# An earlier page fetch, two pools in the other order, and eleven vector instructions on GpSimd, in a chained conditioning, LoRA and paged-attention kernel

## The chip, the cores and the metric

The kernel runs on one core of a Trainium2 chip. The core has engines with a queue of instructions each, which run at the same time and wait for each other through semaphores: TensorE (PE, matrix products and transposes through the identity; its weight loads are listed as PEld), VectorE (DVE), ScalarE (ACT), GpSimd (POOL) and SyncE (SP, which here issues transfers). An engine takes its own queue strictly in order. The metric is the time of one execution in device microseconds (us), the median of several runs; lower is better.

## The reference, cut to what matters

Activations `x` of shape (64, 32, 512) pass four residual layers in float32: a per-sample channel mix, a linear layer with a per-sample LoRA adapter, grouped-query attention over a paged cache, and a second channel mix.

```python
x = x + einsum('bct,bcd->bdt', x, W0[cond])
x = x + (einsum('bsd,od->bso', x, base_w) + base_b + (x @ A[ad]) @ B[ad])
q, k, v = x @ Wq, x @ Wk, x @ Wv            # 32 query heads, 8 key/value heads, 128 each
q, k = rope(rmsnorm(q), pos), rope(rmsnorm(k), pos)
k_all = concat([k_cache[block_table], k])   # 16 pages of 32 rows, then 32 new rows
v_all = concat([v_cache[block_table], v])
scores = where(valid, q @ k_all.T / sqrt(128), -1e30)
x = x + softmax(scores) @ v_all @ Wo
x = x + einsum('bct,bcd->bdt', x, W3[cond])
```

The 64 samples with 32 rows each are 2048 rows of 512.

## The kernel before, in words

**Tiles and steps.** The 2048 rows are 16 tiles `t` of 128 rows (4 samples each). The 8 key/value heads are two groups of 4. A step is one group and one tile, 32 in all; a unit is one sample of a step, 128 in all. A unit has 4 scores (one for each key/value head), and each of these takes one slot of a schedule that is written out by hand: `slot(i)` (L1208) says in which order the work due in slot i is put into the engines' queues. Slots 0 to 511 hold attention. Negative slots hold the layers before it: `First` works on one row tile every two slots, and the first pair of steps is projected beside it.

**Registering.** `at(slot, where, ...)` (L948) registers work for a slot, and `run(slot, where)` puts it out. In each slot the order is "fetch", "pool", the scores of that slot, "out", "pe", "take", "late", "power", a piece of the norm list (`norm_piece`), "turn", "dve", two more pieces, "dve" again, "keep", "act" and "store".

**First layers.** For a tile t, `First` (L387) gathers rows of the tables through GpSimd, mixes and applies the linear layer on TensorE, transposes the result (`turn_out`, `keep_out`) and stores it for later pairs. For each odd t, `sums` (L499) forms four half tiles of 128x256 from the transposed tiles of t-1 and t: the operands `x_12` and `x_34` of a seven-product block multiplication. They are stored by `store_sums`; from tile 13 on, these stores go out on GpSimd's queue (`queue`, L514).

**Projection and norm.** `Block` (L637) multiplies a pair of tiles with a block of weights in seven products. Each of a pair's ten query and key results passes through `Norm` (L708): squares on ScalarE, the power -1/2 on GpSimd (`power`, L723 and L725), then four pieces on VectorE, `scale` (L730), `straight` (L737), `swapped` (L749, two halves) and `sum` (L759), which adds the two rotated parts `rot_a` and `rot_b`. When `sum` has been put out, `norm_piece` (L961) registers the transposition `turn` (L764, `head_ps`) for a later slot, and `keep` copies it to SBUF as qT or kT_new. There are two `rot_a` buffers and one `rot_b` buffer.

**A unit.** Making a `Unit` (L781) asks for the 16 pages of its transposed keys: SP loads page numbers (L794) and issues 16 transfers of 64 KB (L802) into one of two `kT` buffers. `mask` (L817) makes the penalty `pen` of 128x544 on GpSimd. `fetch_values` (L105) gathers the values `v_sb` in four pieces by GpSimd. `scores` (L846, L849) multiplies queries and keys; VectorE adds `pen` and takes the extremum (L854, `sm` and `top`); ScalarE takes the exponential (L865) and the division (L871). `flip` (L888, `pT_ps`) transposes the result, and `values` (L898) multiplies it with the values. Units 0 and 1 are made in slots `ready` and `ready + 3`, with `ready = -6` (L1071); the mask of unit 0 is due in slot -2.

**Pools.** SBUF memory is taken in pools that are opened and closed like a stack. `start` (page rows of the cache and the angles) closes in slot `ready - 1`, and the `kT` pool opens on what it leaves. `first` (all that `First` uses, with the last `x_12` and `x_34`) closes in slot -2; then `pages`, `v`, `attn` (with `pen`, `sm`, `pT`) and the PSUM pool `o` open. A tile in reused memory waits until every earlier user of that memory is done, stores out of it included. Transfers signal on eight semaphores for each kind of queue, which are used in turn.

Of the kernel before, what the change touches and what calls it, by code (L numbers as in the profile page):

```python
# [30 lines left out]
ALU = mybir.AluOpType  # L31
# [14 lines left out]
NT = B * S // P  # L46
# [31 lines left out]
def resid_kernel(  # L78
# [19 lines left out]
    nc = tc.nc  # L98

    def across(ap, n):  # L100

        return bass.AP(tensor=ap.tensor, offset=ap.offset, ap=[[0, P], [1, n]])
# [42 lines left out]
    def rows_of(pool, name, source, n, size, lanes, times=1.0, first=0.0, tag=None):  # L145

        i = pool.tile([P, n], I32, name=name, tag=tag or name)
        for c in range(0, n, 64):
            m = min(n - c, 64)
            f = wpool.tile([P, 64], F32, name=f"{name}_f", tag="w11")  # L150
            nc.vector.tensor_scalar(
                f[:, :m], source[:, c : c + m], float(size), lanes, ALU.mult, ALU.add
            )
            nc.vector.tensor_scalar(i[:, c : c + m], f[:, :m], times, first, ALU.mult, ALU.add)
        return i
# [71 lines left out]
    with ExitStack() as l2:  # L227
# [11 lines left out]
        room = {}  # L239
# [6 lines left out]
        lo, hi = slice(0, NC // 2), slice(NC // 2, NC)  # L246
# [140 lines left out]
        class First:  # L387
# [38 lines left out]
            def add(self):  # L426
                nc.vector.tensor_tensor(self.x, self.ps, lora["bias"], ALU.add)
# [43 lines left out]
            def own_ranks(self):  # L471
                self.hT = first_pool.tile([P, P], F32, name="hT", bufs=2)
                nc.vector.tensor_tensor(self.hT, self.h, lora["mask"][self.t % 2], ALU.mult)
# [25 lines left out]
            def sums(self):  # L499

                p = self.t // 2
                pool = first_pool if p else proj_pool
                a, b = first_of[self.t - 1].x2T, self.x2T
                s = pool.tile([P, NC, P], F32, name="x_12")
                nc.vector.tensor_tensor(s[:, lo], b[:, lo], b[:, hi], ALU.add)
                nc.vector.tensor_tensor(s[:, hi], s[:, lo], a[:, lo], ALU.subtract)
                r = pool.tile([P, NC, P], F32, name="x_34")
                nc.vector.tensor_tensor(r[:, lo], a[:, lo], b[:, lo], ALU.subtract)
                nc.vector.tensor_tensor(r[:, hi], a[:, hi], s[:, hi], ALU.subtract)
                self.s = s, r  # L510
                if p == 0:
                    pair_of[0].x["12"], pair_of[0].x["34"] = s, r
# [18 lines left out]
        def with_identity():  # L531

            lora["eye"] = first_pool.tile([P, S], F32, name="eye")
            nc.vector.tensor_tensor(lora["eye"], ident[:, :S], ident[:, S : 2 * S], ALU.add)
            for j in range(2, NB):
                nc.vector.tensor_tensor(
                    lora["eye"], lora["eye"], ident[:, j * S : (j + 1) * S], ALU.add
                )

        def base_chunk(c):  # L540
            part = lora["base"][:, c, c * P : (c + 1) * P]
            nc.vector.tensor_tensor(part, part, ident, ALU.add)
# [165 lines left out]
        class Norm:  # L708
# [46 lines left out]
                        ALU.mult,  # L755
                    )

            def sum(self):
                nc.vector.tensor_tensor(self.a, self.a, self.b, ALU.add)  # L759

            def turn(self):
                self.tp = ps_t.tile([P, REP, P], F32, name="head_ps", tag="t")
# [185 lines left out]
        def at(slot, where, do, *args):  # L948
            plan.setdefault((slot, where), []).append((do, args))

        def run(slot, where):
            for do, args in plan.pop((slot, where), ()):
                do(*args)
# [7 lines left out]
        def norm_piece(slot):  # L961


            if not pieces or pieces[0][0] > slot or busy.get(slot, 0) >= 2 + (slot % 4 == 1):
                return
            busy[slot] = busy.get(slot, 0) + 1
            _, piece, norm = pieces.pop(0)
            piece()
            if norm:
                slot += 1  # L970
                while slot in turning:
                    slot += 1
                turning.add(slot)
                at(slot, "turn", norm.turn)
                at(slot, "keep", norm.keep)
# [92 lines left out]

        n = KG * len(units)
        begin = -WINDOW - AHEAD - 9  # L1070
        ready = -6  # L1071
        for t in range(NT):
            home = -WINDOW - AHEAD - 6 + 2 * t
            f = [first_of, t]
# [133 lines left out]
        def slot(i):  # L1208
# [30 lines left out]
            run(i, "late")  # L1239
            run(i, "power")  # L1240
            norm_piece(i)
            run(i, "turn")
            if i >= 0:
                run(i, "dve")
            norm_piece(i)
            norm_piece(i)
            run(i, "dve")
            run(i, "keep")
# [4 lines left out]
        with tc.manual_schedule(engines=ENGINES):  # L1253

            lora["base"] = first_pool.tile([P, NC, HID], F32, name="base_sb")
            for c in range(NC):
                nc.scalar.dma_start(out=lora["base"][:, c, :], in_=base_w[:, c, :])
            with_identity()
            adapt_sb = first_pool.tile([P, NT // 2], I32, name="adapt_sb")
            for i in (0, 1):  # L1260
                nc.sync.dma_start(
                    out=adapt_sb[i * P // 2 : (i + 1) * P // 2, :],
                    in_=bass.AP(
                        tensor=ints.tensor,
                        offset=ints.offset + I_ADAPT + i,
                        ap=[[2 * N_INT, P // 2], [2, NT // 2]],
                    ),
                )
            nc.sync.dma_start(out=table, in_=ints[:, I_TABLE:])
            lora["rows"] = rows_of(first_pool, "lora_rows", adapt_sb, NT // 2, RANK, lane16_f)  # L1270

            lora["bias"] = first_pool.tile([P, HID], F32, name="bias_sb")
            slot(begin)
            more = angles()
            next(more)
            nc.gpsimd.dma_start(out=lora["bias"], in_=across(base_b, HID))
            for i in range(begin + 3, begin + 15):
                for _ in range(1 + (begin + 5 < i < begin + 11)):
                    at(i, "store", next, more, None)
            for j in (0, 1):  # L1280
                at(begin + 4, "store", load_kv_weights, 0, 1, j)
                at(begin + 5, "store", load_kv_weights, 0, 0, j)
            for c in range(2 * KG):
                at(begin + 8 + c, "store", load_q_weights, 0, c // 2, c % 2)
            for i in range(begin + 1, begin + 11):
                slot(i)
                if i == begin + 2:
                    lora["mask"] = [own_ranks(0), own_ranks(1)]
                    for c in range(NC):
                        base_chunk(c)  # L1290
                if i == begin + 8:
                    nc.vector.tensor_copy(seq_f, ints_sb[:, I_SEQ : I_SEQ + B])
                    key_i = wpool.tile([P, LA], I32, name="key_i", tag="w9")
                    nc.gpsimd.iota(key_i, pattern=[[1, LA]], base=0, channel_multiplier=0)
                    nc.vector.tensor_copy(key_f, key_i)
                    nc.vector.memset(key_f[:, L:], -BIG)
                    v_rows = rows_of(const, "v_rows", table, B * NC, PSIZE, lane32_f)
            for i in range(begin + 11, n + VLAG):
                if i == ready - 1:
                    start.close()  # L1300
                    room["kT"] = l2.enter_context(tc.tile_pool(name="kT", bufs=2))
                if i == -2:
                    first.close()
                    pages = ExitStack()
                    room["pages"] = pages.enter_context(
                        tc.tile_pool(name="pages", bufs=1, side="right")
                    )
                    room["v"] = l2.enter_context(tc.tile_pool(name="v", bufs=2))
                    room["attn"] = l2.enter_context(tc.tile_pool(name="attn", bufs=2))
                    room["o"] = l2.enter_context(tc.tile_pool(name="ps_o", bufs=1, space=PSUM))  # L1310
                if i == SLOTS * NT + 8:
                    pages.close()
                if i == n - 27:
                    assert not pieces
                    proj.close()
                    o_pools.append(
                        ctx.enter_context(tc.tile_pool(name="o_first", bufs=1, side="right"))
                    )
                slot(i)
            run(n + VLAG, "store")  # L1320
# [7 lines left out]
    with ExitStack() as l3:  # L1328
# [34 lines left out]
        lo, hi = slice(0, HALF), slice(HALF, HID)  # L1363
# [162 lines left out]
```

## Time and profile before

| what | value |
|---|---|
| median of 3 runs | 2446.4 us (2442.44 to 2447.73) |
| the profiled execution's own time | 2447.26 us |
| its span in the profile | 2445.4 us |
| PE busy | 2402.6 us, 98% of the span |
| DVE / ACT / POOL busy | 1649.4 / 1400.8 / 1231.0 us |
| PE busy in 160 to 200 us | 17.46 + 16.50 of 40 us |

The span runs from the first to the last instruction of the program; 1.86 us of the execution lie around it. A line of a timeline gives the start in us, the duration in us, the engine, the source line, the operation, the tiles written and read, how many were merged, and in brackets the engine's idle time before it with what ended that. The end of one line's work may overlap the start of the next on TensorE, where products are pipelined. Attention's slot 0 begins at 181.61 us of the span.

### The profile page before, as it was taken

The page shows a single profiled execution, that of the slowest core. Times are in us where ns is not written, and L with a number is a line of the kernel's source. Part 1 is how long each engine was busy: PE and PEld are TensorE (multiplying, and loading weights), DVE is VectorE, ACT ScalarE, POOL GpSimd, SP SyncE. Part 2 cuts the span into 40 slices and gives each one's busy share as a digit, 9 for nine tenths or more (in the row PEclk, how much of TensorE's full clock was granted, in tenths as well). Part 3 has the DMA queues.
Part 4 walks back from the last instruction along what each step waited for, and adds up shares of the span by engine and source line. Part 5 has one row for each costly group of instructions (what it writes and reads, how often), then busy time and mean ns, then how long its engine had stood idle before and what let it go on. Part 6 is the DMA issues. An engine that isn't in the chain of part 4 may idle for free.

```text
span 2445.4 us, 47109 instructions
## 1 busy us (share of the span) xinstructions
PE 2402.6 (98%) x13792; PEld 1865.4 (76%) x13792; DVE 1649.4 (67%) x3555; ACT 1400.8 (57%) x4005; POOL 1231.0 (50%) x1266
## 2 busy tenths in 40 slices
PE   7999999999999999999999999999999999999999
PEld 4657777777777777777777777777777788888887
DVE  5557777777777777787777777777787756333222
ACT  2246777777777777767777777767677653000000
POOL 3336566656665667665665666566556653000000
PEclk9999999999999999999999999999999999999999
DMA  8776666666766677766666656666667774233221
GB/s 270 250 228 196 192 191 200 190 204 184 207 183 203 189 215 235 235 186 193 173 188 177 189 175 187 178 186 182 181 181 226 248 245 147 105 113 130 87 89 59
DMA packets 461680, 452.09 MB, mean 185 GB/s; under 512 B 67889, under 2 KB 384177, under 8 KB 457841
## 3 DMA queue, kind: packets, MB, share of 16 engines
q1 hardware_dynamic: 405920, 268.95, 36.6%
q0 software_dynamic: 54928, 179.09, 24.3%
q8 instruction: 111, 1.82, 0.3%
q14 instruction: 145, 1.18, 0.2%
q10 hardware_dynamic: 576, 1.05, 0.1%
HBM read 380.73 MB, written 76.55 MB: 187 GB/s over the span
## 4 chain that ended last, share of the span: by engine, by line
PE 92%; DMA 3%; issue 2%; DVE 1%; ACT 1%; SPq 1%; POOL 1%; ACTq 0%; POOLq 0%; DVEq 0%
PE proj_ps L662 22%; PE o_ps L898 17%; PE out_ps L1350 15%; PE s_ps L846 9%; PE pT_ps L888 9%; PE s_ps L849 8%; PE l_ps L479 3%; PE head_ps L764 3%; PE o_ps L911 1%; DMA kT<-kT 1%; DMA o<-oT 1%; PE s_ps L881 1%; SPq L802 1%; PE h_ps L463 1%; PE mix_ps L1368 1%
## 5 line engine op out<-in xcount | busy, mean ns | idle before, releaser
L105 POOL DMA_INDIRECT v_sb<-v,v_rows x512 | 544.2, 1063 | 362.9 <-PE o_ps L898 253.9
L898 PE MATMUL o_ps<-pT,v_sb 128*128 128x128 f32 x4096 | 624.6, 275 | 3.0 <-DVE pT L890 3.0
L898 PEld LDWEIGHTS o_ps<-pT,v_sb 128*128 128x128 f32 x4096 | 577.7, 191 | 32.0 <-DVE pT L890 5.4
L865 ACT ACTIVATE sm<-sm,top 128x544 f32<-128x544 f32 x512 | 380.8, 744 | 332.3 <-DVE top L854 240.7
L854 DVE CUSTOM_DVE_ANT_0 sm<-s_ps,pen 128x544 f32<-128x544 f32 x512 | 369.3, 721 | 112.4 <-PE s_ps L849 99.2
L871 ACT ACTIVATE sm<-sm,share 128x512 f32<-128x512 f32 x512 | 369.8, 722 | 110.5 <-DVE share L870 73.6
L890 DVE COPY pT<-pT_ps 128x512 f32<-128x512 f32 x512 | 353.2, 690 | 66.8 <-PE pT_ps L888 16.3
L846 PE MATMUL s_ps<-kT,qT 128*128 128x288 f32 x1024 | 334.9, 409 | 3.4 <-DMA kT<-kT 1.9
L888 PE MATMUL pT_ps<-ident,sm 128*128 128x128 f32 x2048 | 310.1, 274 | 5.2 <-ACT qT L776 3.7
L674 DVE TENSOR_TENSOR raw<-proj_ps,raw 128x512 f32<-128x512 f32 x332 | 224.4, 688 | 129.3 <-PE proj_ps L662 117.2
L849 PE MATMUL s_ps<-kT,qT 128*128 128x256 f32 x1024 | 304.7, 379 | 4.9 <-issue 2.8
L846 PEld LDWEIGHTS s_ps<-kT,qT 128*128 128x128 f32 x1024 | 179.2, 190 | 151.2 <-issue 127.8
L817 POOL TENSOR_SCALAR pen<-key_f,seq_f 128x544 f32<-128x544 f32 x128 | 283.9, 2218 | 12.5 <-DMA kT<-kT 1.2
L888 PEld LDWEIGHTS pT_ps<-ident,sm 128*128 128x128 f32 x2048 | 239.2, 142 | 9.4 <-ACT qT L776 4.9
L718 ACT ACTIVATE sq<-raw 128x128 f32<-128x128 f32 x640 | 198.5, 310 | 74.0 <-DVE raw L674 56.1
L849 PEld LDWEIGHTS s_ps<-kT,qT 128*128 128x128 f32 x1024 | 194.5, 190 | 59.4 <-issue 5.9
L105 POOL DMA_INDIRECT mix_rows<-in_w,cond_rows x32 | 36.0, 1126 | 349.8 <-DVE mix_diag L170 301.2
L870 DVE RECIPROCAL share<-total 128x1 f32<-128x1 f32 x512 | 83.8, 164 | 180.4 <-ACT sm L865 152.2
L723 POOL TENSOR_SCALAR ss<-ss 128x4 f32<-128x4 f32 x160 | 40.1, 251 | 312.1 <-ACT sq L718 305.9
L1400 ACT COPY p<-out_ps 128x256 f32<-128x256 f32 x7 | 2.6, 373 | 333.1 <-PE out_ps L1350 333.1
L662 PE MATMUL proj_ps<-sum,x 128*128 128x512 f32 x380 | 188.0, 597 | 0.0
L725 POOL TENSOR_TENSOR rstd<-ss,minus_half 128x4 f32<-128x4 f32 x160 | 168.6, 1054 | 13.4
(172 smaller groups left out, 3572.0 us busy)
## 6 DMA issues: line engine op xcount, KB each, us to landing
kT<-kT SPq DMA_DIRECT2D x2048, 64.0 KB
o_in<-o SPq DMA_DIRECT2D x28, 1024.0 KB
o<-oT POOLq DMA_DIRECT2D x69, 256.0 KB
o<-oT SPq DMA_DIRECT2D x58, 256.0 KB
page_rows<-in_kv_cache SPq DMA_DIRECT2D x32, 256.0 KB
v<-in_kv_cache SPq DMA_DIRECT2D x32, 256.0 KB
kT<-page_rows SPq DMA_DIRECT2D x32, 256.0 KB
vn<-raw SPq DMA_DIRECT2D x32, 256.0 KB
```

Source lines behind the costliest of these rows:

```text
L105: nc.gpsimd.indirect_dma_start(out=dst, out_offset=None, in_=table, in_offset=bass.IndirectOffsetOnAxis(ap=index, axis=0),)
L662: nc.tensor.matmul(self.ps, lhsT=self.pair.x[x][:, c if x == "b" else half.start + c, :], rhs=blocks(self.b)[w][:, c, :], start=(c == 0), ...
L817: nc.gpsimd.tensor_scalar(self.pen, key_f, seq_f[:, self.b : self.b + 1], BIG, ALU.is_ge, ALU.mult)
L846: nc.tensor.matmul(ps[:, first:HID], lhsT=q, rhs=self.kT[:, :n1, k, :], start=True, stop=True)
L849: nc.tensor.matmul(ps[:, HID : first + LA], lhsT=q, rhs=self.kT[:, n1:, k, :], start=True, stop=True)
L854: nc.vector.tensor_tensor_reduce(out=sm, in0=ps[:, first : first + LA], in1=self.pen, scale=1.0, scalar=3e38, op0=ALU.add, op1=ALU.min, ac ...
L865: nc.scalar.activation(sm, sm, AF.Exp, bias=top, scale=-1.0, accum_out=total)
L871: nc.scalar.activation(sm[:, :L], sm[:, :L], AF.Copy, scale=share)
L888: nc.tensor.transpose(ps[:, c, :], self.sm[k][:, c * P : (c + 1) * P], ident)
L890: nc.vector.tensor_copy(pT, ps)
L898: nc.tensor.matmul(o_of[self.s, k][:, self.j, :], lhsT=self.v[c][:, k * D : (k + 1) * D], rhs=self.pT[k][:, c, :], start=(self.j == 0 and ...
L1350: nc.tensor.matmul(ps[:, :HALF], lhsT=o[:, i, :], rhs=w[i // REP][:, i % REP, :], start=(i == 0), stop=(i == KG * REP - 1),)
```

## The change

There are four edits.

1. `sums` runs on GpSimd for the last tile (t = 15): four instructions of 128x256. For the other tiles it stays on VectorE.
2. The rotated sum of a `Norm` is put on GpSimd when it is put out in a slot below -1. In the program built from the changed source this is so for seven of the first pair's ten.
3. `ready` becomes -8: unit 0's keys are asked for in slot -8, unit 1's in slot -5, and the `start` pool is closed, and `kT` opened, in slot -9.
4. The `attn` pool is opened before the `v` pool.

```diff
             def sums(self):
...
                 a, b = first_of[self.t - 1].x2T, self.x2T
+                add = (nc.vector if self.t < NT - 1 else nc.gpsimd).tensor_tensor
                 s = pool.tile([P, NC, P], F32, name="x_12")
-                nc.vector.tensor_tensor(s[:, lo], b[:, lo], b[:, hi], ALU.add)
-                nc.vector.tensor_tensor(s[:, hi], s[:, lo], a[:, lo], ALU.subtract)
+                add(s[:, lo], b[:, lo], b[:, hi], ALU.add)
+                add(s[:, hi], s[:, lo], a[:, lo], ALU.subtract)
                 r = pool.tile([P, NC, P], F32, name="x_34")
-                nc.vector.tensor_tensor(r[:, lo], a[:, lo], b[:, lo], ALU.subtract)
-                nc.vector.tensor_tensor(r[:, hi], a[:, hi], s[:, hi], ALU.subtract)
+                add(r[:, lo], a[:, lo], b[:, lo], ALU.subtract)
+                add(r[:, hi], a[:, hi], s[:, hi], ALU.subtract)
...
-            def sum(self):
-                nc.vector.tensor_tensor(self.a, self.a, self.b, ALU.add)
+            def sum(self, engine):
+                engine.tensor_tensor(self.a, self.a, self.b, ALU.add)
...
             _, piece, norm = pieces.pop(0)
-            piece()
+            if norm:
+                piece(nc.gpsimd if slot < -1 else nc.vector)
+            else:
+                piece()
...
-        ready = -6
+        ready = -8
...
+                    room["attn"] = l2.enter_context(tc.tile_pool(name="attn", bufs=2))
                     room["v"] = l2.enter_context(tc.tile_pool(name="v", bufs=2))
-                    room["attn"] = l2.enter_context(tc.tile_pool(name="attn", bufs=2))
```

In the built program the queues read, around the change, as follows. SP: the 16 page transfers of unit 0 stand ahead of the reload of `x_12` (L588) instead of behind it, and those of unit 1 ahead of the reload of `x_34`. GpSimd, from the power of the eighth norm on: power (L723, L725), rotated sum, four x sums, store of the transposed tile 15, two stores of its sums, power, `pen` of unit 0, first gather of values, power, rotated sum, three more gathers, `pen` of unit 1. Before, the same queue reads without the two rotated sums and the four x sums. ScalarE: the first load of the exponential's table (part of L865) is put behind the wait for unit 0's first `top`; before, it stood ahead of that wait.

## The prediction

> **What bounds the kernel now.** I read the page first, then the busy time by stretches, then the idle times of TensorE (PE) in order of time, then GpSimd's timeline. The page has PE busy for 98% of the span and for 92% of the chain that ended last. The stretches (length, then busy us of PE, PEld, DVE, ACT, POOL with their counts, then clock, DMA share, GB/s) show where the edits can matter:
>
> ```profile
> 160.00:180.00 20.00, 17.46 (x65) 8.75 (x64) 16.29 (x33) 8.24 (x31) 8.46 (x14) 1.00 0.54 177
> 180.00:200.00 20.00, 16.50 (x82) 11.61 (x83) 14.79 (x36) 12.17 (x27) 16.95 (x17) 1.00 0.75 220
> ...
> 400.00:500.00 100.00, 99.99 (x619) 77.01 (x619) 75.99 (x169) 72.98 (x211) 62.55 (x64) 1.00 0.65 190
> ```
>
> PE has 6.04 us without work between 160 and 200 us, and 0.01 us between 400 and 500. PE's timeline names the idle times at the entry to attention:
>
> ```profile
> 172.99 0.63 PE L764 MATMUL head_ps<-ident,rot_a 128*128 128x128 f32 x4 [0.48 <-DVE rot_a L759]
> ...
> 176.96 1.98 PE L662 MATMUL proj_ps<-wv,x_a 128*128 128x512 f32 x4 [1.62 <-DVE raw L674]
> 179.05 0.63 PE L764 MATMUL head_ps<-ident,rot_a 128*128 128x128 f32 x4
> 181.61 0.72 PE L846 MATMUL s_ps<-kT,qT 128*128 128x288 f32 x2 [1.93 <-DMA kT<-kT]
> ...
> 189.19 0.63 PE L888 MATMUL pT_ps<-ident,sm 128*128 128x128 f32 x4 [1.37 <-issue]
> ```
>
> They are 0.48 us for a rotated sum, 1.62 us for VectorE, 1.93 us for unit 0's keys, and 1.37 us at 189.19, plus 0.45 us at 186.64 and 0.10 us in small: 5.95 us. That is all that the edits can win here. Every other thing that PE waits for later comes from its own chain, so **what delays PE here delays the end one for one**. The second queue to read is GpSimd's at the same place, since three edits touch it:
>
> ```profile
> 173.36 0.51 POOL L723 TENSOR_SCALAR ss<-ss 128x4 f32<-128x4 f32 x1 [3.00 <-ACT sq L718]
> 173.95 1.20 POOL L725 TENSOR_TENSOR rstd<-ss,minus_half 128x4 f32<-128x4 f32 x1
> 175.12 0.63 POOL L522 DMA_DIRECT2D xT<-x_b  x1
> 175.75 1.08 POOL L526 DMA_DIRECT2D xS<-x  x2
> 177.42 0.51 POOL L723 TENSOR_SCALAR ss<-ss 128x4 f32<-128x4 f32 x1 [0.58 <-ACT sq L718]
> 178.01 1.07 POOL L725 TENSOR_TENSOR rstd<-ss,minus_half 128x4 f32<-128x4 f32 x1
> 180.28 2.54 POOL L817 TENSOR_SCALAR pen<-key_f,seq_f 128x544 f32<-128x544 f32 x1 [1.20 <-DMA kT<-kT]
> 183.10 1.11 POOL L105 DMA_INDIRECT v_sb<-v,v_rows  x1 [0.28 <-DMA kT<-kT]
> 184.28 0.23 POOL L723 TENSOR_SCALAR ss<-ss 128x4 f32<-128x4 f32 x1
> 184.60 1.05 POOL L725 TENSOR_TENSOR rstd<-ss,minus_half 128x4 f32<-128x4 f32 x1
> ```
>
> GpSimd works this off almost without a hole. The 1.20 us ahead of `pen` (L817) is put down to a transfer of keys. The built program tells otherwise: the tile waits for everything that used the closed pool's memory, and last for the second store of the x sums (L526). That is issued until 175.75 + 1.08 = 176.83, and `pen` starts 3.45 us later. The wait stays in the changed program, although the pools trade places.
>
> **The price of the moved work.** No add of this size runs on GpSimd before. The nearest rows are L602 (two inputs, 128 columns), the small L723 (4 columns) and `pen` (544 columns):
>
> ```profile
> L602 POOL TENSOR_TENSOR rot_k<-rot_k,k_turn x60: 454/458/818, 194.4 to 1838.0; 128x128 f32<-128x128 f32 x60
> ```
> ```profile
> L723 POOL TENSOR_SCALAR ss<-ss x160: 224/238/1311, 74.2 to 1940.2; 128x4 f32<-128x4 f32 x160
> ```
> ```profile
> L817 POOL TENSOR_SCALAR pen<-key_f,seq_f x128: 2101/2118/2960, 180.3 to 2028.2; 128x544 f32<-128x544 f32 x128
> L817 POOLq EVENT_SEMAPHORE  x13: 17/43/1576, 178.0 to 2026.3; - x13
> ```
>
> From 230 ns at 4 columns to 458 at 128 the slope is 228/124 = 1.84 ns a column: 1.17 us for 512 columns, 0.69 for 256. That is the low end. By `pen` (2118/544 = 3.9 ns) it is 2.0 and 1.0 us, the high end. VectorE needs 0.69 and 0.42. I take **1.3 and 0.75**, near the low end: L602 is the same kind of operation, and rises to 818 ns at worst beside a busy VectorE, but VectorE waits for most of this stretch.
> [...]
>
> **Keys sooner (edit 3).** SP stands from 155.78 to 168.23 at the reload of `x_12`, and unit 0's 16 page transfers take 169.40 to 179.52 behind it. Moved ahead of it, they use that standstill: about 156 to 168, with 10.1 us of issue. Unit 1's then take about 169 to 179 instead of 180.72 to 190.78. The reload of `x_12` is held by PE until 168.23 anyway and is first used at 189.66; that of `x_34` stays near 179.6 and is used at 200.38. What stands behind on SP comes 10 us sooner. The gain is at most the 1.93 us, and only if nothing else is late there. The two pauses for page numbers change queue place with them and cost nothing, since SP has this slack.
>
> **The first five sums on GpSimd (edit 2).** They end on VectorE at 94.84, 119.95, 135.55, 151.09 and 164.87; PE turns them at 100.69, 125.85, 140.59, 155.84 and 168.03, at least 3.16 us later. On GpSimd each takes 0.6 us more, the third after the power that ends at 135.39. The gathers and stores that they stand ahead of are used several slots later. Zero on the path; if this cover went, each would cost 0.6 us. VectorE is freed of 7 x 0.69 + 4 x 0.42 = 6.5 us, which shows only in the 1.62 us.
>
> **The last two sums and the x sums (edits 1 and 2).** Here GpSimd's queue is the path. Term by term, from the power that ends at 173.95 + 1.20 = 175.15 (its input, the squares, is not moved):
> - sixth rotated sum 1.3: 176.45. Its transposition on PE, 172.99 before, is queued behind it: 3.5 us late.
> - four x sums of 0.75: 179.45. Not needed by PE, but ahead of all that follows.
> - three stores, 0.63 + 1.08: 181.16. The power of 1.66 runs while they land.
> - landing 3.45: 184.61, `pen` 2.54: 187.15.
> - first gather and power, 182.82 to 185.65 before, so 2.83: 189.98.
> - **seventh rotated sum** 1.3: 191.28.
>
> PE's transposition at 179.05 waits for this seventh sum, and unit 0's scores stand behind it in PE's queue. So PE is 191.28 - 179.05 = 12.2 us late there, though the keys have landed long ago. The scores follow 0.44 to 0.47 us behind: 191.75 against 181.61, **10.1 us late**. The 1.93 us of keys and the 0.48 and 1.62 us lie inside this and are not won separately. VectorE's second half of `rot_b` also waits for the seventh sum (one buffer) and is done 0.75 us later, before the scores end.
>
> Then ScalarE. Before, the table load sat in an idle time:
>
> ```profile
> 180.81 1.28 ACT L865 ACT_TABLE_LOAD   x1
> 183.69 0.75 ACT L865 ACTIVATE sm<-sm,top 128x544 f32<-128x544 f32 x1 [1.60 <-DVE top L854]
> ```
>
> In the changed program it stands behind the wait for `top`: 1.28 us more between `top` and the exponential. Everything up to PE's transposition at 189.19 hangs on that: the share, the second `sm`, the copy of qT. So the table load is added in full: 10.0 + 1.3 = **11.3 us**. From there the order is as before and PE has no idle time to take it up (0.04 us in 200 to 220). The pools' exchange (edit 4) by itself is put at nothing: the waits for the closed pool stay, with the store as the last of them.
>
> Sum: span 2445.4 + 11.3 = 2456.7, with the 1.86 us around it 2458.6 for this execution, which is 0.86 us above the median. Against the median, 2446.4 + 11.3 = **2457.7 us**.
>
> **Ends.** Low: 1.17 and 0.69 us for the sums, the landing no longer than the power (1.66), `pen` at its usual 2.12, and the table load hidden. Then 175.15 + 1.17 + 2.76 + 1.71 + 1.66 + 2.12 + 2.83 + 1.17 = 188.57: 9.5 us late at the transposition, 7.4 at the scores, 2453.8. High: 2.0 and 1.0 us, `pen` at its longest (2.96): 175.15 + 2.0 + 4.0 + 1.71 + 3.45 + 2.96 + 2.83 + 2.0 = 194.10, 15.1 late, 13.0 at the scores, 14.3 with the table: 2460.7.
>
> **The rivals.**
> - *The entry's stalls go and nothing takes their place* (not slower). This needs the seventh sum to be done by 179.05 for PE. For it: keys and VectorE are the releasers that the profile names, and both are relieved. Against it: power, stores, landing, `pen` and gather alone, with adds at zero, end at 175.15 + 1.71 + 3.45 + 2.54 + 2.83 = 185.68. Price: 1.93 + 1.62 = 3.55 us won, 2442.9. It decides when the seventh sum is put out ahead of `pen`. Chance 4%.
> - *Part of it is taken up later.* PE idles 2.04 us at 1916.40 for keys and 2.83 us at 1989.39 without a named releaser. If SP, now ahead, brings these sooner, 4.9 us come back: 2457.7 - 4.9 = 2452.8. Against it: there are only two `kT` buffers, so SP's lead ends after two units. Chance 10%.
> - *GpSimd's adds are disturbed by VectorE.* L602 reaches 0.82 us for 128 columns; at that slope from the 4-column row (4.8 ns) the adds take 2.7 and 1.4 us, which adds 2 x 1.4 + 4 x 0.65 = 5.4 us: 2463.1. VectorE stands still while they run, which speaks against it. Chance 6%.
>
> The forecast itself: 80%.
>
> **How the numbers follow.** The predicted time is the forecast's, 2457.7. The forecast's ends are 2453.8 and 2460.7; I widen to 2452.5 and 2461.5, which takes in most of the second rival and leaves under 2 in 10 out. About 0.2%, 4.9 us, is what a measurement can tell here. Slower by more: forecast, third rival and most of the second, 0.93. Within: 0.05, from low ends of the second and a mild form of the first. Faster by more than 4.9 us: 0.02, since even the first rival wins 3.55.
>
> **What would show it.** In the changed profile: PE's idle time ahead of the head transposition before unit 0's first score near 10 us and put to GpSimd; no PE idle time on keys there; GpSimd without holes from about 173 to 191 but for the landing; adds of 1.2 to 1.5 us; the table load behind the first `top`; PE's later stretches as before. Wrong it would be if the seventh sum ran ahead of `pen`, if `pen` started without the store, or if adds took over 2 us.

## The result, and the profile after

The changed kernel takes 2455.55 us (median of six runs, 2451.31 to 2459.27); the kernel before, run beside it, 2443.93 us (six runs, 2439.57 to 2447.73). The ratio is 1.0051, with a 95% interval of 1.0036 to 1.0065: slower by 11.6 us between the medians, 8.8 to 15.9 us by the interval. The profiled execution is the fastest of the six, 2451.31 us with a span of 2449.4 us. Source lines of the changed kernel are one higher than before near these places.

The stretches of the changed kernel (length, then busy us of PE, PEld, DVE, ACT, POOL with their counts, then the clock granted to TensorE, DMA share, GB/s):

```profile
160.00:180.00 20.00, 15.71 (x58) 8.01 (x57) 11.34 (x25) 7.06 (x26) 11.17 (x17) 1.00 0.63 192
180.00:200.00 20.00, 8.61 (x26) 4.84 (x25) 5.16 (x14) 5.85 (x15) 15.62 (x15) 0.74 0.46 130
200.00:220.00 20.00, 18.67 (x95) 13.66 (x95) 15.17 (x33) 12.03 (x33) 8.27 (x10) 0.91 0.50 143
400.00:500.00 100.00, 99.99 (x621) 77.46 (x620) 76.39 (x169) 71.81 (x206) 61.03 (x62) 1.00 0.66 189
```

TensorE's work between 180 and 200 us falls from 16.50 to 8.61 us, while GpSimd is busy for 15.62; between 400 and 500 nothing differs. One column was not expected: the clock stands at 0.74 and 0.91, where it was 1.00 before. TensorE's timeline there (start, duration, line, operation, in brackets the idle time before it and its releaser):

```profile
175.70 0.66 PE L765 MATMUL head_ps<-ident,rot_a 128*128 128x128 f32 x4 [3.50 <-POOL rot_a L760]
...
178.86 1.98 PE L663 MATMUL proj_ps<-wv,x_a 128*128 128x512 f32 x4 [0.79 <-DVE raw L675]
190.87 1.11 PE L765 MATMUL head_ps<-ident,rot_a 128*128 128x128 f32 x4 [10.02 <-POOL rot_a L760]
191.78 1.17 PE L847 MATMUL s_ps<-kT,qT 128*128 128x288 f32 x2
```

Ahead of unit 0's first score TensorE waits 10.02 us, and the releaser is the rotated sum on GpSimd. The wait for keys is gone. The transposition of four heads then takes 1.11 us instead of 0.63, and the score 1.17 instead of 0.72: the granted clock reads 0.50 over them (from 184.25 to 194.49 us). GpSimd's timeline shows what made the sum late:

```profile
174.40 1.25 POOL L760 TENSOR_TENSOR rot_a<-rot_a,rot_b 128x512 f32<-128x512 f32 x1
175.61 0.73 POOL L506 TENSOR_TENSOR x<-x_b 128x256 f32<-128x256 f32 x1
...
179.08 1.08 POOL L527 DMA_DIRECT2D xS<-x  x2
...
184.62 2.12 POOL L818 TENSOR_SCALAR pen<-key_f,seq_f 128x544 f32<-128x544 f32 x1 [2.31 <-DMA x<-xS]
187.03 1.11 POOL L105 DMA_INDIRECT v_sb<-v,v_rows  x1 [0.28 <-issue]
...
189.56 1.25 POOL L760 TENSOR_TENSOR rot_a<-rot_a,rot_b 128x512 f32<-128x512 f32 x1
```

The queue is worked off in its order with one hole, the wait of `pen`. The seventh sum at 189.56 stands behind all of it. ScalarE's rows show the last link of the chain:

```profile
194.63 1.28 ACT L866 ACT_TABLE_LOAD   x1 [1.54 <-issue]
195.93 0.75 ACT L866 ACTIVATE sm<-sm,top 128x544 f32<-128x544 f32 x1
```

The table load starts when the first `top` is there, and the exponential waits for it.

### The profile page after: what moved, and what is told of

The parts are those of the page before. It is cut to its first block, busy times and chain, and to the rows that moved or that the text cites. A ratio compares the mean times of both kernels' runs of the same rounds, so it can differ in the third digit from the quotient of the medians.

```text
span 2449.4 us, 47105 instructions
## 1 busy us (share of the span) xinstructions
PE 2402.5 (98%) x13792; PEld 1866.1 (76%) x13792; DVE 1645.0 (67%) x3544; ACT 1400.7 (57%) x4005; POOL 1242.4 (51%) x1277
## 4 chain that ended last, share of the span: by engine, by line
PE 93%; issue 2%; DMA 1%; ACT 1%; DVE 1%; SPq 1%; POOL 1%; ACTq 0%; DVEq 0%; POOLq 0%
PE proj_ps L663 23%; PE o_ps L899 18%; PE out_ps L1354 15%; PE s_ps L847 10%; PE pT_ps L889 9%; PE s_ps L850 9%; PE head_ps L765 3%; PE l_ps L479 2%; PE o_ps L912 1%; PE s_ps L882 1%; PE mix_ps L1372 1%; SPq L803 1%; PE h_ps L463 1%; DMA o<-oT 1%; PE x1T_ps L448 0%
```

## The experiments

Each kernel was run beside the kernel before on the same chip; the ratio is to that one. The edits are against the changed kernel unless said otherwise.

### The kernel before once more

A second profile of the unchanged kernel before.

> The kernel before once more, unchanged, for a second profile. It tells whether TensorE's idle times near 1916 us (2.04 us) and 1989 us (2.83 us), which the changed kernel's profile lacks, belong to the kernel or to one execution. If to the kernel, both are there again within 0.5 us; if to the execution, at least one is gone or elsewhere. The entry to attention should be the same within 0.5 us: first sm near 182.9 us.

It took 2438.22 us, with a span of 2436.4, so 9.0 us less than in the first profile. The entry to attention is about the same, but the late idle times are not. The first profile of the kernel before had, late in attention:

```profile
1916.40 0.67 PE L849 MATMUL s_ps<-kT,qT 128*128 128x256 f32 x2 [2.04 <-DMA kT<-kT]
...
1989.39 0.67 PE L849 MATMUL s_ps<-kT,qT 128*128 128x256 f32 x2 [2.83 <-issue]
```

The second has:

```profile
1928.32 0.67 PE L849 MATMUL s_ps<-kT,qT 128*128 128x256 f32 x2 [1.08 <-DMA kT<-kT]
...
1996.62 0.67 PE L849 MATMUL s_ps<-kT,qT 128*128 128x256 f32 x2 [1.41 <-DMA kT<-kT]
```

So these waits belong to the execution. This matters for reading lags. The table below gives, for the same TensorE instruction, its start in a kernel's profile minus its start in this second profile of the kernel before (us), at six places of that profile:

```
kernel                    170    189    200    600   1900   2400
before, first profile    -0.1   -0.1   -1.0   -0.5    1.6    9.0
keys_and_pools            0.3    0.0    0.7    0.7    1.5    6.4
stores_on_act            -0.2    0.6    0.3    0.4    0.5    0.2
seventh_back              0.1    4.6    3.7    3.6    3.1    3.0
seventh_first             0.2    6.0    5.1    5.1    4.8    3.6
xsums_back               -1.1    6.9    6.0    6.0    6.6    5.0
after, second profile     0.6   12.0   11.1   11.1   11.3   10.5
table_early              -0.3   10.8    9.9   10.5   10.5   12.1
after, first profile     -0.4   12.2   12.9   12.9   12.9   13.0
```

The lag of every kernel but the first row's is made before 200 us and stands within 1 us of that at 1900. (Of the two kernels with unneeded products, which the table leaves out, the one with nine has 9.7 us at 200 and at 1900 us, the one with twenty 21.8 and 24.4.) Against the first profile alone one would have read that the changed kernel takes up some 10 us late, from 12.9 + 1.0 = 13.9 us at 200 us to 13.0 - 9.0 = 4.0 at the end; that was the first profile's own loss.

### Earlier keys and exchanged pools alone

```diff
-                add = (nc.vector if self.t < NT - 1 else nc.gpsimd).tensor_tensor
+                add = nc.vector.tensor_tensor
...
-                piece(nc.gpsimd if slot < -1 else nc.vector)
+                piece(nc.vector)
```

> Edits 3 and 4 alone: the keys asked for sooner and the pools exchanged, all sums back on VectorE. If the delay comes from GpSimd's queue, as the prediction says, it is gone: TensorE no longer waits for keys before unit 0's first score, VectorE's first sm still waits for pen, which starts 3 to 4 us after the last store of the x sums as before, so between 0 us and 1 us is lost against the kernel before (2443.9 to 2445), and ScalarE's table load is again ahead of the wait for top. If the earlier keys or the exchanged pools were the cause, it keeps most of the 11.6 us: 2452 or more.

2438.09 us against 2437.57, ratio 0.9999 (0.9990 to 1.0008). TensorE's and VectorE's timelines of this kernel:

```profile
179.93 0.65 PE L847 MATMUL s_ps<-kT,qT 128*128 128x288 f32 x2
...
183.72 0.75 PE L847 MATMUL s_ps<-kT,qT 128*128 128x288 f32 x2 [1.33 <-DVE top L855]
...
189.18 1.07 PE L889 MATMUL pT_ps<-ident,sm 128*128 128x128 f32 x4 [1.37 <-issue]
```
```profile
182.93 0.72 DVE L855 CUSTOM_DVE_ANT_0 sm<-s_ps,pen 128x544 f32<-128x544 f32 x1 [1.17 <-POOL pen L818]
```

The first score starts without a wait, 1.7 us sooner. But VectorE can't go on before `pen`, which has not moved, so the second score waits for `top`, and `pT` stands at 189.18, where it stood at 189.19 before. The 1.93 us were covered by `pen`: the keys were not the last thing to be late. Nor does `pen` itself wait for them: unit 0's transfers are issued from 159.73 to 170.19 us here and from 169.40 to 179.52 before, and `pen` starts at 180.34 and 180.28.

### The seventh sum back on VectorE

```diff
-                piece(nc.gpsimd if slot < -1 else nc.vector)
+                piece(nc.gpsimd if slot < -2 else nc.vector)
```

> The changed kernel, with only the seventh rotated sum (the one that stands behind pen) back on VectorE. By the queue theory TensorE's transposition no longer waits for GpSimd there (10.0 us of idle time in the changed kernel go), but pen still ends near 186.7 us, so VectorE's first sm starts near 186.8 instead of 193.8; the table load is hidden. Remaining loss against the kernel before about 4 us (2447 to 2449), and TensorE's clock stays at full speed or nearly. If instead GpSimd's adds slow VectorE down by sharing memory with it, one add less changes little: 10 us or more stay.

2441.72 us against 2437.57, ratio 1.0018 (1.0009 to 1.0027), 4.2 us between the medians. TensorE's timeline:

```profile
176.21 1.11 PE L765 MATMUL head_ps<-ident,rot_a 128*128 128x128 f32 x4 [3.49 <-POOL rot_a L760]
...
185.10 0.86 PE L765 MATMUL head_ps<-ident,rot_a 128*128 128x128 f32 x4
```

The second transposition no longer waits for GpSimd. What is left is the sixth sum and the later `pen`, which VectorE's first `sm` waits for (1.17 us). One add of 1.25 us in the wrong place of a queue is thus worth 11.6 - 4.2 = 7.4 us of the loss, as a difference of medians from separate runs. Not all of it is the wait itself: ScalarE's table load starts at 187.08 here, ahead of the first `top`, so the exponential follows `top` 0.8 us sooner than in the changed kernel. One expectation missed: the clock did not stay whole. It was at half from 175.37 to 185.61 us (the granted clock is 0.88 in the mean over 160 to 180 us and 0.86 over 180 to 200), which is why the second transposition stands at 185.10; `pen`, which ends at 187.04, covers that.

### The x sums back on VectorE

```diff
-                add = (nc.vector if self.t < NT - 1 else nc.gpsimd).tensor_tensor
+                add = nc.vector.tensor_tensor
```

> The changed kernel with the four x sums of the last tile back on VectorE (edit 1 undone), the rotated sums still on GpSimd. By the queue theory everything behind them on GpSimd comes 4 x 0.73 = 2.9 us sooner, so the seventh sum ends near 187.5 us instead of 190.8, and the table load stands ahead of the wait for top again (1.28 us): the loss against the kernel before is 6.5 to 8.5 us where the changed kernel has 11.6. If the x sums were the whole cause, the loss is gone; if they had no part in it, it stays at 11 to 12 us.

2445.96 us against 2437.57, ratio 1.0036 (1.0024 to 1.0048), 8.4 us between the medians; so the four x sums are worth 3.2 us as a difference of medians. Two things go with them: their own 2.85 us on GpSimd's queue, and the table load of 1.28 us, which stands ahead of the first `top` again, as was expected:

```profile
189.20 1.28 ACT L866 ACT_TABLE_LOAD   x1
190.69 0.75 ACT L866 ACTIVATE sm<-sm,top 128x544 f32<-128x544 f32 x1 [0.21 <-DVE top L855]
```

Together that would be 4.1 us; these runs don't resolve the difference. TensorE's wait for the seventh sum is now:

```profile
186.96 1.12 PE L765 MATMUL head_ps<-ident,rot_a 128*128 128x128 f32 x4 [4.06 <-POOL rot_a L760]
```

### The seventh sum ahead of the penalty

The changed kernel, with the mask of unit 0 and its first gather one slot later. On GpSimd's queue the third power and the seventh sum then stand ahead of them. ScalarE's table load moves too, as its rows below show.

```diff
-            at(KG * (u - 1) + 1 if u else -2, "pool", call, unit_of, u, "mask")
+            at(KG * (u - 1) + 1 if u else -1, "pool", call, unit_of, u, "mask")
...
-                at(KG * u - 2 + c, "pool", call, unit_of, u, "fetch_values")
+                at(max(KG * u - 2 + c, -1), "pool", call, unit_of, u, "fetch_values")
```

> The changed kernel with one thing exchanged on GpSimd's queue: the mask of unit 0 (pen) and its first gather of values are put out one slot later, so that the third power and the seventh rotated sum stand ahead of them. All other queues are the same. The theory (the seventh sum is late because it stands behind pen, which waits for the landing of the x sums' second store): the seventh sum starts near 183.7 us right behind the power and ends near 184.9, TensorE waits some 4 us for it instead of 10.0, pen starts right behind it (the store has landed by then), and the first sm at 187.1 to 187.7 instead of 193.8. Some 6 us of the 11.6 come back: a loss of 5 to 6 us, ratio 1.0022. The rival (the seventh sum is late for its own inputs, the pieces on VectorE or the squares, not for its place): it starts at 187 us or later, and the loss stays above 9 us (1.0037 or more). A second rival (pen, now behind the sum, sets the end instead): the first sm follows pen, not the scores, and stands at 188 or later.

2445.49 us against 2438.18 (12 and 18 runs), ratio 1.0028 (1.0016 to 1.0039): a loss of 6.8 us by the ratio, a little over what was expected. By the lags at 200 us it is 5.1, against 12.9 and 11.1 in the two profiles of the changed kernel. GpSimd's timeline:

```profile
183.26 1.04 POOL L726 TENSOR_TENSOR rstd<-ss,minus_half 128x4 f32<-128x4 f32 x1
184.28 1.26 POOL L760 TENSOR_TENSOR rot_a<-rot_a,rot_b 128x512 f32<-128x512 f32 x1
185.64 2.60 POOL L818 TENSOR_SCALAR pen<-key_f,seq_f 128x544 f32<-128x544 f32 x1
```

The seventh sum starts the moment the power ahead of it is done, so its inputs were there; TensorE waits 4.19 us for it, not 10.02, and turns it at 185.60 instead of 190.87. The place in the queue is the cause. What came back holds one thing more, which the expectation left out: the table load stands ahead of the first `top` in this kernel.

```profile
187.84 1.28 ACT L866 ACT_TABLE_LOAD   x1
189.43 0.75 ACT L866 ACTIVATE sm<-sm,top 128x544 f32<-128x544 f32 x1 [0.31 <-DVE top L855]
```

So about 1.3 us belong to the table load. The first `sm` began at 188.66 and not at 187.1 to 187.7:

```profile
188.66 0.72 DVE L855 CUSTOM_DVE_ANT_0 sm<-s_ps,pen 128x544 f32<-128x544 f32 x1 [2.33 <-PE s_ps L850]
```

That is the time of the second rival, but not its cause: `pen` took 2.60 us and ended at 188.24, and the scores, at half clock, ended 0.28 us later (187.46 + 1.06 = 188.52). With the 0.62 us that this score takes in the kernel before, at a granted clock of 1.00, they would have ended at 188.08 by estimate, and `pen` would have been the last.

### The table load made early

```diff
+        def first_exp():
+            early_exp = small.tile([P, 1], F32, name="share")
+            nc.scalar.activation(early_exp, minus_half, AF.Exp)
+
+        at(-5, "act", first_exp)
```

> The changed kernel with one more ScalarE instruction, an exponential of a 128x1 tile put out in slot -5, so that the exponential's table is loaded long before the first top. The theory (the table load lies in full on the path at the entry): the load of 1.28 us is gone from between the first top and the first exponential, TensorE turns pT 1.3 us sooner than in the changed kernel, and the loss against the kernel before is 10.3 us instead of 11.6 (ratio 1.0042). The rival (another engine's work, the second sm on VectorE or the copy of qT, ends as late as the table load and hides it): TensorE's idle time ahead of pT stays at 1.3 us, and the loss stays at 11.6 us (ratio 1.0048). The difference of the two is at the edge of what the comparison resolves; the timeline at the entry decides.

2454.93 us against 2441.43, ratio 1.0060 (1.0042 to 1.0077): the times don't tell 1.3 us, and here lie on the wrong side. The timelines tell it. ScalarE goes straight from `top` to the exponential, and TensorE's `pT` follows:

```profile
194.63 0.75 ACT L866 ACTIVATE sm<-sm,top 128x544 f32<-128x544 f32 x1 [1.56 <-issue]
```
```profile
190.85 1.11 PE L765 MATMUL head_ps<-ident,rot_a 128*128 128x128 f32 x4 [9.85 <-POOL rot_a L760]
...
200.07 0.66 PE L889 MATMUL pT_ps<-ident,sm 128*128 128x128 f32 x4 [1.33 <-ACT qT L777]
```

From the late transposition to `pT` it is 200.07 - 190.85 = 9.22 us. In the two profiles of the changed kernel it is 201.36 - 190.87 and 201.19 - 190.70, both 10.49. The difference, 1.27 us, is the table load. The lag of this execution grows again late (from 8.9 us near 2010 to 12.1 behind 2040), in waits that differ from one execution to the next.

### TensorE kept busy while it waits

The changed kernel with unneeded products of 128x512, put on TensorE in slot -1 ahead of the last projection. Their result is not read.

```diff
+        def fill():
+            idle_ps = room["o"].tile([P, NB, P], F32, name="o_ps", tag="o3")
+            for _ in range(FILL):
+                nc.tensor.matmul(
+                    idle_ps.rearrange("p j c -> p (j c)"),
+                    lhsT=ident,
+                    rhs=key_f[:, :L],
...
+        at(-1, "pe", fill)
```

First with FILL = 20:

> The changed kernel with 20 unneeded products of 128x512 (some 10 us at 0.495 us each) put on TensorE in the slot -1, ahead of the last projection before the late transposition, so that TensorE works through the time in which it waits for the seventh rotated sum. Nothing reads their result. The theory (the clock's half rate from 184 to 194 us follows the 10 us without work, and costs some 2.5 us on top of the wait): the clock stays whole through the entry, TensorE lags 11 to 12 us behind the kernel before at 200 us instead of 13.8, and the kernel is 1.5 to 2.5 us faster than the changed one though it does more work (ratio 1.0038 against 1.0048). The rival (the half rate belongs to the execution or the place, not to the idle time): the half rate is there again, lag 13.8 us and ratio 1.0048 as in the changed kernel. A third (the products are slower than 0.5 us, and push the late transposition): transposition later than 191 us, ratio above 1.0048.

2462.87 us against 2441.43, ratio 1.0083 (1.0063 to 1.0102). I had mis-sized the products. Each shows as two instructions:

```profile
181.49 18.07 PE L1077 MATMUL o_ps<-key_f,ident 128*128 128x512 f32 x40
...
201.12 0.60 PE L766 MATMUL head_ps<-ident,rot_a 128*128 128x128 f32 x4
```

They took 18.07 us and pushed the transposition to 201.12, the third case of the expectation; nothing follows from its time. The clock was whole at the transposition, as the theory has it (0.60 us instead of 1.11). It was at half from 176.15 to 182.97 us, from within the wait of 3.50 us for the sixth sum on, and again for 3.41 us from 210.28 (in the mean 0.90, 0.93 and 0.91 over the three 20 us from 160 us on). Then with FILL = 9:

> As the first kernel with unneeded products, with 9 instead of 20 (the 20 took 18.1 us, 0.9 us each, and pushed the late transposition to 201 us): 8.1 us of products, which end with the last projection near 188 us, ahead of the seventh sum. The theory (the half rate near 184 to 194 us comes of TensorE's 10 us without work): the head transposition after the seventh sum takes 0.6 instead of 1.1 us, the first two scores 0.65 and 0.59 instead of 1.17 and 1.06, and TensorE's lag at the first pT is 0.5 to 0.8 us less than in the two profiles of the changed kernel with the same start of the transposition. The time then lies at 11 us above before (1.0045), which the comparison can hardly tell from 1.0048; the durations decide. The rival (the half rate belongs to the place and not to the idle time): 1.11, 1.17 and 1.06 us again. A half rate right behind the first wait of 3.5 us, at 176 to 180 us, may come in either case.

2448.84 us against 2438.18, ratio 1.0043 (1.0026 to 1.0060), not told apart from the changed kernel's. TensorE's timeline:

```profile
177.82 7.89 PE L1077 MATMUL o_ps<-key_f,ident 128*128 128x512 f32 x18
...
190.06 0.66 PE L766 MATMUL head_ps<-ident,rot_a 128*128 128x128 f32 x4 [2.63 <-POOL rot_a L761]
190.55 0.68 PE L848 MATMUL s_ps<-kT,qT 128*128 128x288 f32 x2
191.04 1.05 PE L851 MATMUL s_ps<-kT,qT 128*128 128x256 f32 x2
...
199.65 0.66 PE L890 MATMUL pT_ps<-ident,sm 128*128 128x128 f32 x4 [1.32 <-ACT qT L778]
```

The transposition and the first score run at full clock here (0.66 and 0.68 us); from 191.04 on, after an idle time of 2.63 us, there is one stretch at half clock, of 3.41 us instead of 10.24 (a granted clock of 0.91 in the mean over 180 to 200 us instead of 0.74). From the transposition to `pT` it is 9.59 us instead of 10.49. So the half clock of the transposition and the first score came with the idle time ahead of them, and cost about 0.9 us. This is one execution; the last section takes all of them together.

### The last stores issued by ScalarE

Earlier keys and exchanged pools alone, with the last tile's three stores on ScalarE's queue. It was meant to be faster than both kernels.

```diff
-                return nc.sync if self.t < NT - 3 else nc.gpsimd
+                return nc.sync if self.t < NT - 3 else nc.gpsimd if self.t < NT - 1 else nc.scalar
```

> Keys sooner and pools exchanged, all sums on VectorE, and the last tile's three stores (its transpose and the two of its x sums) issued by ScalarE instead of GpSimd. The theory (pen waits on GpSimd's queue for these stores, and then for their landing; with the keys early, the first sm waits 1.17 us for pen): GpSimd comes to pen without 1.7 us of issue in front of it, pen starts near 179.1 instead of 180.3, the first sm is then released by TensorE's scores, and some 1 us is won: ratio 0.9996 against the kernel before. Rival 1 (the landing decides, wherever it is issued): ScalarE issues them later than GpSimd did, behind its squares, pen starts at 180.3 or later, and nothing is won or up to 2 us lost (ratio 1.0000 to 1.0008). Rival 2: the 1.7 us of issue on ScalarE delay its squares and with them the eighth norm, so that TensorE waits for a head transposition: 1 to 2 us slower (1.0004 to 1.0008).

2444.17 us against 2441.43, ratio 1.0009 (1.0000 to 1.0018): no gain. The first rival holds. The last issue on ScalarE's queue, then GpSimd's timeline:

```profile
177.56 0.33 ACTq L527 DMA_DIRECT2D xS<-x  x1
```
```profile
177.97 1.06 POOL L726 TENSOR_TENSOR rstd<-ss,minus_half 128x4 f32<-128x4 f32 x1
181.46 2.12 POOL L818 TENSOR_SCALAR pen<-key_f,seq_f 128x544 f32<-128x544 f32 x1 [2.44 <-DMA kT<-kT]
```

ScalarE issues the second store behind its squares, until 177.89. GpSimd is free at 179.03, with nothing to issue, yet `pen` starts at 181.46, 3.57 us behind the end of that issue. `pen` moved with the store to another queue. From the end of the last of these issues to `pen` it is 3.45 us before, 3.08 with the keys and pools alone, 3.35 with the x sums back, 3.57 here, 3.92 with the seventh sum back, and 4.46 and 3.30 in the two profiles of the changed kernel. In the four other profiles in which GpSimd was free then (the second one before, the early table load, the two with unneeded products) it is 3.22 to 4.28. The row's bracket names a transfer of keys in eight of these eleven, other loads in two and the store itself in one, and is not to be followed.

### The changed kernel once more

> The changed kernel once more, unchanged, for a second profile. The theory (the wait for the seventh sum and the half clock after it belong to the kernel, the late idle times near 1916 and 1989 us to the execution): TensorE waits 10.0 us within 0.3 for the seventh sum, the clock is halved again for 6 to 14 us in the 20 us after it began to wait, and TensorE's idle time between 1900 and 2040 us differs by 1 us or more from that of the first profile. The rival (the half clock was chance): the wait is there, the clock is whole. For the late idle times the rival is that they are the same within 0.3 us, in which case the smaller lag at the end belongs to the change.

2448.86 us, span 2446.9. The wait for the seventh sum is 7.48 us here, not 10.0, so that number of the expectation missed; the transposition stands at the same place all the same:

```profile
176.70 1.12 PE L765 MATMUL head_ps<-ident,rot_a 128*128 128x128 f32 x4 [3.50 <-POOL rot_a L760]
177.61 2.85 PE L663 MATMUL proj_ps<-sum,x_b 128*128 128x512 f32 x4
181.24 1.98 PE L663 MATMUL proj_ps<-wv,x_a 128*128 128x512 f32 x4 [0.78 <-DVE raw L675]
190.70 1.11 PE L765 MATMUL head_ps<-ident,rot_a 128*128 128x128 f32 x4 [7.48 <-POOL rot_a L760]
```

A stretch of half clock began at the end of the first wait of 3.50 us, at 176.14, and made TensorE's work slower inside a time that it would have waited through anyway. A second, of 10.24 us, came again in the longer wait (in the mean 0.91 over 160 to 180 us, 0.74 over 180 to 200). Late in attention this execution has a wait of 1.42 us near 2005 us that the first profile lacks; between 1900 and 2040 us TensorE idles 6.95 us, against 5.89 there.

## Why the prediction was right

**The number.** Predicted were 2457.7 us, 11.3 above the kernel before; measured are 2455.55, 11.6 above. The time lies 2.15 us lower because the kernel before, run beside it, took 2443.93 us and not the 2446.4 that the prediction started from.

**The bound.** That a delay of TensorE at the entry delays the end one for one held: the lags made before 200 us are there at 1900 us in every changed kernel of the table, within 1 us.

**The chain on GpSimd.** It was predicted term by term, and the order of its terms was right. Against the rows of the two profiles after (us; sums and stores from start to start):

```
term                          predicted   first   second
power ends                       175.15  174.40   175.40
sixth rotated sum                  1.3     1.21     1.21
four x sums                        3.0     2.85     2.84
three stores                       1.71    1.70     1.71
landing, to the start of pen       3.45    4.46     3.30
pen                                2.54    2.12     2.12
first gather and power             2.83    2.82     2.82
seventh rotated sum                1.3     1.25     1.25
seventh sum ends                 191.28  190.81   190.65
```

Two terms were mis-sized, the landing and `pen`, in opposite ways in the first profile. The price of the adds, bounded only by distant rows, came out at 1.25 and 0.73 us for the 1.3 and 0.75 taken.

**`pen` waits for the second store, not the keys.** Shown by `pen`'s start, which follows the end of that issue by 3.1 to 4.5 us in eleven profiles, with the store on either of two queues, and which did not move when the keys came some 9.5 us sooner. What sets the time of one landing was not looked into.

**Keys sooner won nothing, the pools' exchange cost nothing.** Both together gave 0.9999. Tried apart they were not. The prediction named the condition ("only if nothing else is late there"), and `pen` was.

**First five sums hidden.** No row of TensorE before the sixth names a rotated sum on GpSimd as releaser; its three waits on line 760 are 3.50, 10.02 and one of 0.78 us for VectorE.

**From the sum to `pT`.** Scores 10.1 us late predicted, 191.78 - 181.61 = 10.2 found. The table load of 1.28 us was added in full, and 1.27 showed. Those make 11.4 us. What the prediction lacked is the clock: the half rate made the stretch from the first score to `pT` 201.36 - 191.78 = 9.58 us, where 7.58 + 1.28 = 8.86 had been implied, and in the first profile one more stretch of it at 201.3 us added 1.7 us to the lag (12.17 us at the first `pT`, 13.83 at the score behind it). In the second profile that last one was missing. Measured from their own lags at 170 us, the two profiles are 13.3 and 10.5 us late at 200 us against the second profile of the kernel before, and 14.2 and 11.4 against the first, from which the prediction was worked out. So the predicted 11.3 us fit the second profile of the changed kernel, and are 3 us short of its first. Where they fit, two errors made up for each other: from the end of the power to the end of the seventh sum the queue took 190.65 - 175.40 = 15.25 us, where 16.13 had been predicted, mostly by a shorter `pen`, and the half clock, which was missing, added 0.45 us at the transposition and 0.72 from the first score to `pT`. The closeness of the total is in part luck.

**The rivals.** That the stalls go and nothing takes their place needed the seventh sum ahead of `pen`, as the prediction said. With that order the loss fell by some 5 us, 1.3 of them by the table load, but did not vanish, because the sixth sum, the x sums and the stores still stand ahead of the seventh on that queue. That part of the loss is taken up later looked true against the first profile of before and fell with the second. Disturbed adds did not occur at the entry: 1.25 us, with VectorE idle for 9.44 us meanwhile; the longest of the seven took 1.65.

The sixth sum and the first five were not tried apart from the rest. No version beat the kernel before by an amount that these runs can tell.

## What to carry to other kernels

Work that is moved to an engine "with time to spare" costs what its place in that engine's queue makes it wait for, not its duration: 1.25 us of addition cost some 7 us behind a wait for a transfer, 0.8 of them by a table load that moved with it, and some 5 us of the loss came back when the sum was put ahead of that wait. Look at every queue after such an exchange: the table load on ScalarE changed its place without having been touched. Before a wait is removed, ask which other wait ends just behind it; here the keys' 1.93 us were covered by the penalty. Take two profiles of the same kernel before reading where a lag is made up.

## What the runs showed of the hardware

TensorE's clock fell to half in or behind some of its idle times. In the first profile of the changed kernel the granted clock reads 0.50 for 10.24 us from 184.25 us, within the idle 10.02 us, and for 3.41 us from 201.31 us, at the end of an idle 1.33 us. In its second profile it was at half from 176.14 us, within the idle 3.50 us (0.91 in the mean over 160 to 180 us), and for 10.24 us from 186.38 us, within the idle 7.48 us. In the first profile of the kernel before it reads 0.50 for 3.41 us from 1990.30 us, behind its idle 2.83 us.

The length of the idle time alone did not tell the cases apart. Behind the wait for the sixth sum, 3.49 to 3.54 us in eight profiles, the transposition took 0.66 us in five (the first of the changed kernel, and those with the table load early, the seventh sum first, the x sums back and the nine products) and 1.11 or 1.12 us in three (the second of the changed kernel, and those with the seventh sum back and the twenty products). Behind the waits for the seventh sum of 4.06, 4.19, 7.48, 9.85 and 10.02 us it took 1.11 or 1.12 us, and behind the 2.63 us with the nine products 0.66, with half clock from 191.04 us on. Shorter idle times had it too: 2.35 us with the stores on ScalarE, where the score behind it took 1.02 us and the same product at 179.47 us 0.65, and 1.37 us with the keys and pools alone, where `pT` took 1.07 us, while behind the same 1.37 us in the kernel before it took 0.63. What decides it was not shown.

What the half rate cost depended on what it fell on: nothing that shows where TensorE would have waited anyway (the late transposition stands at 190.70 us in the second profile of the changed kernel, with half clock from 176.14 us, and at 190.87 in the first, without it there), 0.9 us at the transposition and first score, and 1.7 us where TensorE worked through the whole stretch: from the first `pT` to the score behind it are 205.21 - 201.36 = 3.85 us in the first profile of the changed kernel and 193.04 - 189.18 = 3.86 with the keys and pools alone, where the kernel before takes 191.38 - 189.19 = 2.19.
